# Second pass of a four-layer graph kernel: a fixed order for VectorE and ScalarE over each period of seven products

## The chip, the cores and the metric

The kernel runs on one core of one Trainium2 chip. The metric is the device time of one execution in microseconds (us). Six runs of the kernel before gave 2606.01 to 2609.18, with a median of 2606.47.

## What is computed

The input is `x` (128 x 128 x 256, float32) and one 128 x 128 adjacency matrix. Four layers follow, each of the form `x = x + layer(relu(layernorm(x)))`: a gated graph layer, attention, three graph convolutions, and a layer with two batch norms. The change touches only the second half of the last layer:

```python
agg = jnp.einsum('nm,bmd->bnd', A_hat, features)
x = agg.reshape(-1, d)
h = jax.nn.relu(_batchnorm(x @ W1.T + b1, g1, be1))
out = h @ W2.T + b2
out = _batchnorm(out, g2, be2)
return out.reshape(b, n, -1)
```

Each batch norm needs the mean and variance over all 16384 rows before any row can go on. So the kernel has three stages here: a first pass that ends with `x @ W1.T` of every group, the second pass (normalise, relu, multiply by `W2`, gather statistics) and a final pass (second batch norm, transpose back, add `x`, write out).

## The kernel before

The 128 batches are worked on in 32 groups of four, so that one group is a matrix of 512 rows. After the first pass the pre-activations of 31 groups lie in DRAM as tiles `Z[g]` (128 partitions x 4 chunks x 512 columns), and group 31 is still in SBUF (tiles `zo`). `ORDER` (line 839) is 31, 0, 1, ..., 30. Here n is the place in that order, so n = 0 is group 31 and n = 31 is group 30.

**Loads.** `load_z` (line 843) fetches one group, 1 MB, into one of three buffers `zi` through SyncE's queue. The load for place n+4 is written at the end of place n's turn (line 923) and takes the buffer of place n+1, so it can start only when the last product of place n+1 has read that buffer.

**One group.** `second(g)` (line 859) is a generator, and each `yield` is a step. Four steps apply the first batch norm and the relu in place, one chunk each, on ScalarE (line 868; `relu0` to `relu3`). One step makes sums of quarters of the tile on VectorE (lines 872 to 874). With the quarters a11, a21, a12, a22 these are s1 = a21 + a22, then a21 = a11 - a21, then s2 = s1 - a11, and later, behind product 1, a12 = a12 - s2 (line 884). The matrix product itself is done by a scheme of seven products of half size in place of eight. `seven` (line 412) issues them in the order 0, 1, 4, 5, 2, 6, 3 into three PSUM banks x, y and z:

| step | product into bank | reads | then |
|---|---|---|---|
| 1 | 0 into x | a11 | ScalarE copies x out: `t1` (line 419) |
| 2 | 1 into y | a12 | VectorE a12 = a12 - s2, and the add `o00` = y + t1 (line 894) |
| 3 | 4 into z | s1 | ScalarE copies z out: `t5` (line 419) |
| 4 | 5 onto x | s2 | ScalarE copies x out: `t2` (line 419) |
| 5 | 2 onto z | new a12 | VectorE `o01` = z + t2 |
| 6 | 6 onto x | new a21 | VectorE `o11` = x + t5; half j = 1 is complete: its statistics `S1` (line 897) |
| 7 | 3 onto x | a22 | ScalarE copies the result out: `o10` (line 892); half j = 0 is complete: its statistics `S0` |

Product 5 goes onto bank x and so needs `t1` done; product 2 goes onto z and needs `t5` done; product 6 needs `t2`, and product 3 needs `o11`. A product is four matmul records in the profile (two matmuls of 128 x 256, each in two records), all of line 879.

**Two groups at a time.** The main loop (lines 911 to 925) runs `now`, whose product 0 is already issued, and `then`, the next group. It takes five steps of `now` (products 1, 4, 5, 2, 6) with one preparing step of `then` behind each (four relus, then the sums), then product 0 of `then`, then product 3 of `now`. TensorE's order as written is thus, with a dash for the next group, 1, 4, 5, 2, 6, 0', 3 and again 1', 4', and so on: a period of seven products.

**What sets the order.** The program is written as one stream, and the framework chooses the order of the instructions on each engine when it builds the program: among those whose inputs it takes to be ready, the one that is written first. An engine works through its list in that order, and an instruction that waits holds up all behind it. `tc.keep_in_program_order` puts an instruction behind the one written just before it on the same engine, and adds no wait. In the second pass of the kernel before nothing has it.

**Around it.** `bn_affine` (line 797) turns the statistics into a scale and a shift. For the second batch norm `bn_part` (line 742) aggregates those of the first 31 places into `most2` (line 914, two `BATCH_NORM_AGGREGATE` of line 746), and those of the last place into `last2` (line 936). The final pass (lines 939 to 961) cannot start before both.

Of the kernel before, what the change touches and what calls it, by code (L numbers as in the profile page):

```python
# [9 lines left out]
AF = mybir.ActivationFunctionType  # L10
ALU = mybir.AluOpType
# [11 lines left out]
def kernel(  # L23
# [39 lines left out]
    nc = tc.nc  # L63
    B, N, D = x.shape
    G = 4
    NG = B // G
    T = G * N
    DC = D // P
# [5 lines left out]
    FC = F1 // P  # L74
# [60 lines left out]
    stats2 = const.tile([P, DC, NG, 6], FP, name="stats2")  # L135
# [50 lines left out]
    for v in (b1, g1, be1, b2, g2, be2):  # L186
        k = v.shape[0] // P
# [123 lines left out]
    LAST = NG - 1  # L311
# [100 lines left out]
    def seven(product, put, shape, name, pool=None):  # L412

        def kept(pb, i):
            t = (pool or w).tile(shape, FP, tag="kept", name=f"{name}_t{i}", bufs=6)
            nc.scalar.copy(t, pb)  # L419
            return t  # L420

        px = bank(shape, f"{name}_x")
        product(0, px, True)
        t1 = kept(px, 1)
        yield
        py = bank(shape, f"{name}_y")
        product(1, py, True)
        put((0, 0), py, t1)
        yield
        pz = bank(shape, f"{name}_z")  # L430
        product(4, pz, True)
        t5 = kept(pz, 5)
        yield
        product(5, px, False)
        t2 = kept(px, 2)
        yield
        product(2, pz, False)
        put((0, 1), pz, t2)
        yield
        product(6, px, False)  # L440
        put((1, 1), px, t5)
        yield
        product(3, px, False)
        put((1, 0), px, None)
        yield
# [296 lines left out]
    def bn_part(stats, nch, groups, name):  # L742

        mv = const.tile([P, nch, 2], FP, name=f"mv_{name}")
        for j in range(nch):
            nc.vector.bn_aggr(mv[:, j, :], stats[:, j, groups].rearrange("p g s -> p (g s)"))
        return mv[:, :, 0], mv[:, :, 1]
# [49 lines left out]
    def bn_affine(most, last, nch, gam, bet, name, bias, n):  # L797


        (mean, var), (mean1, var1) = most, last  # L800
        share = n / NG
        d = const.tile([P, nch], FP, name=f"d_{name}")
        nc.vector.tensor_tensor(d, mean1, mean, ALU.subtract)
        nc.vector.scalar_tensor_tensor(mean, d, share, mean, ALU.mult, ALU.add)
        nc.vector.tensor_tensor(mean, mean, bias, ALU.add)
        nc.vector.scalar_tensor_tensor(d, d, share * (1.0 - share), d, ALU.mult, ALU.mult)
        nc.vector.scalar_tensor_tensor(d, var, 1.0 - share, d, ALU.mult, ALU.add)
        nc.vector.scalar_tensor_tensor(var, var1, share, d, ALU.mult, ALU.add)
        sc = const.tile([P, nch], FP, name=f"sc_{name}")
        inv_sqrt(sc, var, BN_EPS)  # L810
        nc.vector.tensor_tensor(sc, sc, gam, ALU.mult)
        sh = const.tile([P, nch], FP, name=f"sh_{name}")
        nc.vector.tensor_tensor(sh, mean, sc, ALU.mult)
        nc.vector.tensor_tensor(sh, bet, sh, ALU.subtract)
        part = const.tile([P, nch], FP, name=f"part_{name}")
        nc.vector.tensor_tensor(part, bias, sc, ALU.mult)
        nc.vector.tensor_tensor(sh, sh, part, ALU.add)
        return sc, sh
# [4 lines left out]
    O = [keep.tile([P, DC, T], FP, name=f"o_{g}") for g in range(NG)]  # L823
# [19 lines left out]
    def load_z(n):  # L843
        z = zin.tile([P, FC, T], FP, tag="zi", name=f"zi_{ORDER[n]}")
        nc.sync.dma_start(z, Z[ORDER[n]])
        ZT[ORDER[n]] = [z[:, :FC // 2, :], z[:, FC // 2 :, :]]

    def load_x3(g, queue=nc.gpsimd):
        k = g % ROOM
        if IN_PASS <= k < IN_Z:  # L850
            if (k - IN_PASS) % 2 == 0:
                pair = zin.tile([P, 2, G, D], FP, tag="zi", name=f"x3i_{g}")
                R[g], R[g + 1] = pair[:, 0], pair[:, 1]
        else:
            pool, tag = (x3p, "x3") if k < OWN else (zp, "z") if k < IN_PASS else (late, "x3l")
            R[g] = pool.tile([P, G, D], FP, tag=tag, name=f"x3i_{g}")
        queue.dma_start(R[g], X3[g].rearrange("(p r) d -> p r d", r=G))

    def second(g):

        zl, zr = ZT[g]
        ex = zw.tile([P, 2, FC // 2, T // 2], FP, tag="zs", name=f"zs_{g}")
        a11, a21, a12, a22 = (z[:, :, i * T // 2 : (i + 1) * T // 2] for z in (zl, zr) for i in range(2))
        s1, s2 = ex[:, 0], ex[:, 1]
        a_r = a11, a12, a12, a22, s1, s2, a21
        for j in range(FC):
            z = ZT[g][j // 2][:, j % 2, :]
            nc.scalar.activation(  # L868
                z, z, AF.Relu, bias=sh1[:, j : j + 1], scale=sc1[:, j : j + 1],
            )  # L870
            yield
        nc.vector.tensor_tensor(s1, a21, a22, ALU.add)
        nc.vector.tensor_tensor(a21, a11, a21, ALU.subtract)
        nc.vector.tensor_tensor(s2, s1, a11, ALU.subtract)
        yield

        def product(r, pb, first):
            for c in range(FC // 2):
                nc.tensor.matmul(  # L879
                    pb, BW2R[r][:, c, :], a_r[r][:, c, :],  # L880
                    start=(first and c == 0), stop=(c == FC // 2 - 1), skip_group_check=True,
                )
            if r == 1:
                nc.vector.tensor_tensor(a12, a12, s2, ALU.subtract)

        done = []

        def put(ij, pb, other):
            i, j = ij
            dst = O[g][:, j, i * T // 2 : (i + 1) * T // 2]  # L890
            if other is None:
                nc.scalar.copy(dst, pb)
            else:
                nc.vector.tensor_tensor(dst, pb, other, ALU.add)
            done.append(j)
            if done.count(j) == 2:
                nc.vector.bn_stats(stats2[:, j, (g + 1) % NG, :], O[g][:, j, :])

        yield from seven(product, put, [P, T // 2], f"po_{g}", zw)

    load_z(1)
# [2 lines left out]
    for n in range(2, 1 + AT_ONCE):  # L904
        load_z(n)
    sc1, sh1 = bn_affine(most1, last1, FC, g1_c, be1_c, "bn1", b1_c, 2)
    PREPARE = FC + 1
    now = second(LAST)
    for _ in range(PREPARE + 1):
        next(now)  # L910
    for n, g in enumerate(ORDER):
        then = second(ORDER[n + 1]) if n + 1 < NG else iter(())
        if n + 1 == NG:
            most2 = bn_part(stats2, DC, slice(LAST), "most2")
        for _ in range(PREPARE):
            next(now)
            next(then, None)
        next(then, None)
        for _ in now:
            pass  # L920
        now = then
        if n + 1 + AT_ONCE < NG:
            load_z(n + 1 + AT_ONCE)
        if n % 4 == 3 and n // 4 < IN_PASS:
            load_x3(n // 4, nc.sync)
# [7 lines left out]

    for g in range(IN_Z, ROOM):
        load_x3(g, nc.sync)
    last2 = bn_part(stats2, DC, slice(LAST, NG), "last2")
    sc2, sh2 = bn_affine(most2, last2, DC, g2_c, be2_c, "bn2", b2_c, 1)
    rows_out = out.rearrange("b (k r) d -> (b k) r d", r=G)
    for g in range(NG):
        x3 = R[g]  # L940
        for i in range(DC):
            nc.scalar.activation(
                O[g][:, i, :], O[g][:, i, :], AF.Identity,
                bias=sh2[:, i : i + 1], scale=sc2[:, i : i + 1],
# [51 lines left out]
```

## Time and profile before

| what | value |
|---|---|
| median of six runs | 2606.47 us |
| the profiled execution's own time | 2606.73 us |
| its span, first to last instruction | 2604.7 us |
| time around the span | 2.0 us |
| TensorE clock granted in the second pass | 1.00 |
| first and last matmul of the second pass (line 879) start | 2330.02 and 2532.57 us |
| records of line 879 | 896 = 32 groups x 7 products x 4 |
| last instruction of VectorE before the final pass ends | 2537.1 us |

The second pass is thus some 203 of the 2605 us. A line of the timeline or of the chain begins with the start and the duration in us. In the timeline follow engine, line of code, operation, what is written and read, the shape and a count, and in brackets the idle time of the engine before it and what ended it. PEld is the loading of weights for a matmul, which may run beside the matmul before it.

### The profile page before, as it was taken

The numbers are of one execution on the slowest core, as the hardware profiler recorded it, in microseconds if no ns is written. First come the engines' busy times: TensorE is split into PE (matmuls) and PEld (weight loads), VectorE is DVE, ScalarE is ACT, GpSimd is POOL, SyncE is SP. The second block draws the span as 40 slices with busy tenths as digits, with TensorE's granted clock in tenths as the row PEclk, the third lists the DMA queues.
The fourth block names the chain that finished last, engine by engine and source line by source line (L and its number), as shares of the span: only waits on it lengthen the run. The fifth ranks groups of instructions, "written<-read, shape, count | busy, mean of one in ns | idle before, by whom it ended". The sixth has DMA issues, their size and how long they took to land.

```text
span 2604.7 us, 40680 instructions
## 1 busy us (share of the span) xinstructions
PE 2539.4 (97%) x15281; PEld 2283.5 (88%) x15281; DVE 1913.8 (73%) x4820; ACT 1283.7 (49%) x2575; POOL 292.1 (11%) x581
## 2 busy tenths in 40 slices
PE   5999999999999999999999999999999999999995
PEld 4899999999999999999999999999999999888875
DVE  6777777777777777777777777777777776567776
ACT  4544454444445544454444444554445444346656
POOL 2110111111110111111111110111011111000001
PEclk8999999999999999999999999999999999999998
DMA  3000000000000000000000000000000000035449
GB/s 133 15 33 33 33 25 25 33 33 34 33 25 25 33 33 33 33 33 17 33 33 33 33 25 25 33 33 33 33 33 25 25 25 25 25 136 181 175 171 394
DMA packets 49560, 143.06 MB, mean 55 GB/s; under 512 B 4162, under 2 KB 23124, under 8 KB 45396
## 3 DMA queue, kind: packets, MB, share of 16 engines
q1 hardware_dynamic: 42164, 116.48, 12.1%
q0 software_dynamic: 6480, 23.60, 2.5%
q8 instruction: 120, 1.97, 0.3%
q14 instruction: 76, 0.62, 0.1%
q10 hardware_dynamic: 720, 0.39, 0.1%
HBM read 73.48 MB, written 66.98 MB: 54 GB/s over the span
## 4 chain that ended last, share of the span: by engine, by line
PE 91%; DMA 3%; DVE 2%; ACT 2%; issue 1%; POOL 1%; ACTq 0%; DVEq 0%; SPq 0%; POOLq 0%
PE p_x L404 17%; PE p_x L387 9%; PE p_z L404 8%; PE pmu L359 4%; PE p_z L387 4%; PE pz_x L404 4%; PE p_y L404 4%; PE pu_x L387 4%; PE po_x L879 3%; PE pg L359 2%; PE ps L577 2%; PE pm L497 2%; PE p_y L387 2%; PE pqv_x L534 2%; PE pr L707 2%; PE py L607 2%
## 5 line engine op out<-in xcount | busy, mean ns | idle before, releaser
L345 ACT ACTIVATE h<-x,sh,rs 128x256 f32<-128x256 f32 x512 | 269.0, 590 | 370.7 <-POOL sh L342 370.7
L404 PE MATMUL p_x<-uT,w 128*128 128x256 f32 x1024 | 242.2, 379 | 0.0
L679 ACT ACTIVATE h2T<-h2T 128x512 f32<-128x512 f32 x192 | 120.6, 628 | 229.0 <-DVE h2T L678 228.5
L404 PEld LDWEIGHTS p_x<-uT,w 128*128 128x128 f32 x1024 | 189.7, 190 | 23.2
L334 DVE BATCH_NORM_STATS2 st<-x 128x6 f32<-128x256 f32 x512 | 191.2, 415 | 3.6 <-DMA x<-in_x_dram 1.5
L338 POOL TENSOR_SCALAR rs<-mv 128x4 f32<-128x4 f32 (+1 forms) x131 | 31.3, 239 | 1394.6 <-ACT h2T L679 1026.7
L456 DVE SCALAR_TENSOR_TENSOR gs<-h,gw 128x256 f32<-128x256 f32 x384 | 161.2, 420 | 33.6 <-ACT h L345 27.6
L419 ACT COPY p_t<-p_x 128x512 f32<-128x512 f32 (+1 forms) x192 | 96.8, 504 | 108.3 <-PE p_x L404 101.5
L339 POOL TENSOR_TENSOR rs<-rs,nhalf 128x4 f32<-128x4 f32 (+1 forms) x131 | 149.7, 1143 | 0.0
L359 PEld LDWEIGHTS pmu<-a2T,u 128*128 128x128 f32 x1024 | 119.4, 192 | 15.3 <-issue 15.1
L387 PEld LDWEIGHTS p_x<-w,h2T 128*128 128x128 f32 x1024 | 124.3, 192 | 3.3
L387 PE MATMUL p_x<-w,h2T 128*128 128x128 f32 x1024 | 124.6, 275 | 0.0
L632 ACT ACTIVATE u<-u 128x512 f32<-128x512 f32 x93 | 58.7, 631 | 133.8 <-DVE u L631 133.8
L868 ACT ACTIVATE zi<-zi,sh_bn,sc_bn 128x512 f32<-128x512 f32 x124 | 97.4, 813 | 49.0 <-DMA zi<-z 39.0
L404 PE MATMUL p_x<-us,w_s 128*128 128x256 f32 x512 | 121.3, 379 | 0.0
L404 PE MATMUL p_z<-us,w 128*128 128x256 f32 x512 | 121.2, 379 | 0.0
L404 PE MATMUL p_x<-uT,w_s 128*128 128x256 f32 x512 | 121.1, 379 | 0.0
L404 PE MATMUL p_y<-uT,w 128*128 128x256 f32 x512 | 121.0, 379 | 0.0
L404 PE MATMUL p_z<-us,w_s 128*128 128x256 f32 x512 | 120.9, 379 | 0.0
L359 PE MATMUL pmu<-a2T,u 128*128 128x128 f32 x1024 | 119.5, 275 | 0.0
L708 DVE TENSOR_TENSOR x<-pr,x 128x512 f32<-128x512 f32 x64 | 43.7, 683 | 90.4 <-PE pr L707 90.4
L404 PEld LDWEIGHTS p_z<-us,w 128*128 128x128 f32 x512 | 97.2, 190 | 13.6 <-ACT p_t L419 0.4
(300 smaller groups left out, 6181.2 us busy)
## 6 DMA issues: line engine op xcount, KB each, us to landing
z<-zo SPq DMA_DIRECT2D x62, 512.0 KB, 2.6
zi<-z SPq DMA_DIRECT2D x31, 1024.0 KB, 4.9
x<-x POOLq DMA_DIRECT2D x32, 512.0 KB, 3.4
x<-in_x_dram SPq DMA_DIRECT2D x31, 512.0 KB, 4.0
out_dram<-x3i SPq DMA_DIRECT2D x30, 512.0 KB, 13.7
x3i<-x SPq DMA_DIRECT2D x19, 512.0 KB, 5.1
x3i<-x POOLq DMA_DIRECT2D x13, 512.0 KB, 11.4
w<-in_L_gnn_W_dram SPq DMA_DIRECT2D x1, 2048.0 KB
```

The lines of the kernel that those rows point to most:

```text
L334: nc.vector.bn_stats(st[:, k, :], xt[:, b, :])
L339: nc.gpsimd.tensor_tensor(rs, rs, nhalf[:, :n], ALU.pow)
L345: nc.scalar.activation(h[:, b, :], xt[:, b, :], AF.Relu, bias=sh[:, k : k + 1], scale=rs[:, k : k + 1])
L359: nc.tensor.matmul(pm[:, k, :], src[:, b, c * P : (c + 1) * P], aT, start=True, stop=True)
L387: nc.tensor.matmul(pb[:, rr, :], a_r[r][:, c, rr * P : (rr + 1) * P], b_r[r][:, c, :wide], start=(first and rr == 0 and c == 0), stop=(c = ...
L404: nc.tensor.matmul(pb[:, jj, :], b_r[r][:, c, at : at + P], a_r[r][:, c, :], start=(first and jj == 0 and c == 0), stop=(c == nk - 1), ski ...
L419: nc.scalar.copy(t, pb)
L456: nc.vector.scalar_tensor_tensor(gs, h[:, b, :], 1.0, gw[:, i, :], ALU.mult, ALU.mult, accum_out=gl[:, k, i : i + 1],)
L632: nc.scalar.activation(dst, dst, AF.Relu)
L679: nc.scalar.activation(dst, dst, AF.Relu)
L868: nc.scalar.activation(z, z, AF.Relu, bias=sh1[:, j : j + 1], scale=sc1[:, j : j + 1],)
L879: nc.tensor.matmul(pb, BW2R[r][:, c, :], a_r[r][:, c, :], start=(first and c == 0), stop=(c == FC // 2 - 1), skip_group_check=True,)
```

## The change

No instruction is added or removed, and first and final pass are untouched. In the second pass:

- The relus, sums, adds, the subtraction behind product 1 and the statistics are kept in program order. The copies `t1`, `t5`, `t2` and `o10` are not marked themselves.
- The order in which they are written is another. Of the next group's preparing steps one relu comes behind product 1, none behind 4, two behind 5, one behind 2, and the sums behind 6 (`AHEAD_AT`).
- The sums are written s1, s2, a21 in place of s1, a21, s2.
- The statistics are put on a list, `TOLD`, and issued by `tell()` behind each step: `S1` directly behind `o11`, and `S0` of the group before behind `o00` of this one. A last `tell()` stands ahead of `last2`.
- `most2` is written behind the first step of the last turn, not ahead of it.

So ScalarE's list over a period reads relu0'', t5', t2', relu1'', relu2'', relu3'', t1'', o10', and VectorE's reads o11, S1, s1', s2', a21', a12', o00', S0, o01' (two dashes: the group after the next).

```diff
+    TOLD = []
+
+    def tell():
+
+        for g, j in TOLD:
+            tc.keep_in_program_order(
+                nc.vector.bn_stats(stats2[:, j, (g + 1) % NG, :], O[g][:, j, :])
+            )
+        TOLD.clear()
+
+    def in_order(*operands):
+        tc.keep_in_program_order(nc.vector.tensor_tensor(*operands))
...
-            nc.scalar.activation(
-                z, z, AF.Relu, bias=sh1[:, j : j + 1], scale=sc1[:, j : j + 1],
+
+            tc.keep_in_program_order(
+                nc.scalar.activation(
+                    z, z, AF.Relu, bias=sh1[:, j : j + 1], scale=sc1[:, j : j + 1],
+                )
             )
             yield
-        nc.vector.tensor_tensor(s1, a21, a22, ALU.add)
-        nc.vector.tensor_tensor(a21, a11, a21, ALU.subtract)
-        nc.vector.tensor_tensor(s2, s1, a11, ALU.subtract)
+        in_order(s1, a21, a22, ALU.add)
+        in_order(s2, s1, a11, ALU.subtract)
+        in_order(a21, a11, a21, ALU.subtract)
...
-                nc.vector.tensor_tensor(a12, a12, s2, ALU.subtract)
+                in_order(a12, a12, s2, ALU.subtract)
...
-                nc.vector.tensor_tensor(dst, pb, other, ALU.add)
+                in_order(dst, pb, other, ALU.add)
             done.append(j)
             if done.count(j) == 2:
-                nc.vector.bn_stats(stats2[:, j, (g + 1) % NG, :], O[g][:, j, :])
+                TOLD.append((g, j))
...
-    PREPARE = FC + 1
+    PREPARE, AHEAD_AT = FC + 1, (1, 0, 2, 1, 1)
...
-        if n + 1 == NG:
-            most2 = bn_part(stats2, DC, slice(LAST), "most2")
-        for _ in range(PREPARE):
+        for k in range(PREPARE):
             next(now)
-            next(then, None)
+            tell()
+            if k == 0 and n + 1 == NG:
+                most2 = bn_part(stats2, DC, slice(LAST), "most2")
+            for _ in range(AHEAD_AT[k]):
+                next(then, None)
         next(then, None)
...
+    tell()
     last2 = bn_part(stats2, DC, slice(LAST, NG), "last2")
```

## The prediction

> **What bounds the kernel now.** I read the page first (one core, clock 1.00 in the second pass), then the matmul start times of line 879, then the waits of 2340 to 2520 us, the timeline of single periods, and the chain.
>
> The busy share says little: TensorE reads as busy all through the pass, because records of 0.38 us overlap. The distance from one record to the next says more. Of 895 distances in the pass, 809 are 0.216 us and the rest longer. The pass takes 895 x 0.2158 = 193.2 us plus 9.4 us of delays. A period of 28 records is 6.04 us without delay, and from the fifth product 4 (2358.08) to the last but one (2520.89) it is on average 162.81 / 26 = 6.26. So TensorE bounds the pass, with 0.22 us per period lost to hand-overs. These are the waits that matter (who waits, for whom, total us, times, longest):
>
> ```profile
> ACT zi L868 <- DMA zi<-z: 39.0, 21, 2.1
> DVE stats L897 <- ACT o L892: 30.7, 27, 1.5
> ...
> PEld po_z L879 <- ACT po_t L419: 7.1, 23, 0.5
> ...
> PEld po_x L879 <- DVE o L894: 5.1, 26, 0.2
> ```
>
> The two large ones lie on engines with time to spare. The two small ones are TensorE's: product 2 (po_z) waits for the copy t5, product 3 (po_x) for the add o11. Here is one such period:
>
> ```profile
> 2502.03 1.03 PE L879 MATMUL po_z<-zs,bw2s_late 128*128 128x256 f32 x4
> 2502.07 1.52 ACT L868 ACTIVATE zi<-zi,sh_bn,sc_bn 128x512 f32<-128x512 f32 x2
> ...
> 2503.49 0.35 ACT L419 COPY po_t<-po_z 128x256 f32<-128x256 f32 x1
> ...
> 2503.90 0.73 PEld L879 LDWEIGHTS po_z<-zi,bw2T 128*128 128x128 f32 x4 [0.39 <-ACT po_t L419]
> 2503.90 1.13 PE L879 MATMUL po_z<-zi,bw2T 128*128 128x256 f32 x4
> ```
>
> Product 4 starts at 2502.03, and two relus sit in front of t5 in ScalarE's list. t5 starts 1.46 us behind product 4, and product 2 comes 1.87 behind it where 8 x 0.216 = 1.73 was possible: 0.14 lost, and 0.10 more inside product 2, whose weights were not loaded ahead. In another period nothing is in front of t5:
>
> ```profile
> 2345.91 1.03 PE L879 MATMUL po_z<-zs,bw2s_late 128*128 128x256 f32 x4
> ...
> 2346.97 0.37 ACT L419 COPY po_t<-po_z 128x256 f32<-128x256 f32 x1 [0.92 <-PE po_z L879]
> ...
> 2347.63 1.03 PE L879 MATMUL po_z<-zi,bw2T 128*128 128x256 f32 x4
> ```
>
> t5 starts at +1.06, and product 2 at +1.72, with no loss. Over all periods in which the order of products held, a t5 up to +1.19 costs nothing, +1.27 costs 0.06, +1.34 costs 0.11, +1.46 costs 0.24. The same holds for o11: at +1.06 behind product 6 (two periods) no loss at product 3, at +1.21 (most periods, behind the sum s2 in VectorE's list) 0.06.
>
> Why the relus stand there, the chain shows:
>
> ```profile
> 2501.39 4.81 DMA zi<-z
> ...
> 2506.29 0.51 ACT zi L868
> 2506.80 0.21 issue
> 2507.01 0.35 ACT po_t L419
> ```
>
> relu0 starts the moment its load lands. The load was issued 1.15 us behind the start of the product 3 that frees its buffer. So there is a loop over two periods: product 3 of n-3, load (5.96 to relu0), four relus with two copies between (3.3), t5 (0.4), product 2 to product 3 of n-1 (2.6). It gives 12.3 / 2 = 6.13, close to the 6.26 seen.
>
> **The change, part by part.** No instruction comes or goes; only places in two lists change. I lay the new lists over a period by rows. Time 0 is the start of product 6; then 0' 0.86, 3 1.73, 1' 2.59, 4' 3.45, 5' 4.32, 2' 5.18, next 6 6.04. A copy or add can start 1.06 after its product starts. Neighbours follow at 0.72 (relu), 0.61 (VectorE, 512 wide), 0.33 (256 wide), 0.72 to 0.79 where one reads the result before it.
>
> *ScalarE*: t1' 1.92, o10 2.79, relu0'' 3.1 to 3.9, t5' 4.51 (nothing ahead since 3.9), t2' 5.38, relu1'' 5.70, relu2'' 6.42, relu3'' to 7.96, t1'' 7.97. So t5 and t2 start at +1.06 in each period. What the order makes late: relu3 ends 0.2 before s1 wants it; relu1 ends (6.52) before product 0'' (6.91). relu0'' now waits for o10, not for the load, which lands at product 3 + 5.9 = 1.6 in this frame, 1.5 ahead of its turn. Queued behind a relu0 that waits would be t5, t2 and all of ScalarE; the cover is those 1.5 us, and a lateness beyond 0.6 more would reach product 2.
>
> *VectorE*: o11 1.06, S1 1.52, s1' 2.13 to 2.82 (product 4' at 3.45), s2' 2.88 to 3.56 (product 5' at 4.32), a21' 3.49, a12' 4.10 to 4.78 (product 2' at 5.18), o00' 4.7, S0 5.03 to 5.72, o01' 6.24 with 0.5 idle before it, o11' 7.10, that is +1.06. S0 no longer waits for o10 (3.15); that wait of 30.7 us cost nothing, as a12 behind it was done 0.3 before product 2. SyncE's queue, the loads and their buffers are as before.
>
> *Sum.* Start: s2 directly behind s1 lets product 5 start at 2333.67, not 2334.18, and product 2 at 2334.82 (a12 done), not 2335.38. The second product 4 comes at 2339.23, not 2339.80: **-0.57**. Then 30 periods at 6.044 are 181.3 us, where the trace has 2527.68 - 2339.80 = 187.9: **-6.57**. The end: the two aggregates of `most2` now stand between S0 and o01 of the last turn.
>
> ```profile
> 2526.56 0.99 DVE L746 BATCH_NORM_AGGREGATE mv_most<-stats 128x2 f32<-128x186 f32 x1
> ...
> 2528.63 0.98 DVE L746 BATCH_NORM_AGGREGATE mv_most<-stats 128x2 f32<-128x186 f32 x1
> ...
> 2531.34 0.42 DVE L894 TENSOR_TENSOR o<-po_x,po_t 128x256 f32<-128x256 f32 x1 [0.37 <-PE po_x L879]
> 2531.82 1.13 PE L879 MATMUL po_x<-zi,bw2s_late 128*128 128x256 f32 x4 [0.52 <-DVE o L894]
> ```
>
> Before, they ended ahead of o00, and o11 started at once (1.06 behind product 6 at 2530.28). Now S0 ends at 5.69, the aggregates at 6.7 and 7.6, o01 starts at 7.54 and o11 at 7.88 in place of 7.10: **+0.79**, as nothing stands between product 6 and product 3 in the last turn. If the builder moves one aggregate forward into idle time, it is nothing. What follows (statistics, `last2`, final pass) keeps its order and starts earlier by as much, its loads too, since they wait for the pass's buffers: one to one.
>
> Sum -6.35, so 2600.4. Pauses that the profile puts down to "issue" (1.57 and 1.42 us on ScalarE, 0.34 on VectorE) now fall into lists with some 0.5 us of room at a time. They cost between nothing, as ScalarE's two did (their periods took 6.13 and 6.18), and 2 us; I take 0.4, near the trace's own case. **-5.9 against the profiled execution's 2606.73: 2600.8**, 5.7 under the median, since that execution lies 0.26 above it.
>
> The Trainium skill ("Runtime: NRT & Kernel Launch", Instruction fetch mechanics) says that instructions are fetched in sequence while earlier ones run, so that the fetch is mostly hidden. If these pauses are fetches, that rule would take nothing for them, and the sum would be 2600.4; the trace's 1.57 us says that not all is hidden.
>
> **Rivals.** 0.2% is 5.2 us, about what a measurement of this kernel can tell from no change.
>
> 1. *One hand-over stays a little late.* t5, t2 and o11 have only 0.13 us between +1.06 and the first loss. If each period keeps one loss of 0.10 (the row of product 2), 30 x 0.10 = 3.0: 2603.8. For it: the thin margin. Against it: t2 started at +1.06 in 27 periods and delayed product 6 in none.
>
> 2. *The gap belongs to the buffers, not to the list.* If a load into a freed buffer stays what ends last, the period stays 6.26: -0.57 + 0.79, 2606.9. For it: relu0 waits for the load in 21 periods. Against it: the loop with one relu ahead of t5 is 5.96 + 0.72 + 0.4 + 2.6 = 9.7 over two periods, less than 12.1. The Trainium skill ("Perfetto Trace Analysis", Optimization Strategy) speaks for this rival: a gap that repeats for a stretch can mean that there is no room for the next tile. The trace agrees that the gap repeats and that the load waits for a buffer; it does not show that the gap needs the buffer.
>
> 3. *Slower: TensorE's own order slips.* The change binds two engines, not TensorE. Where the builder takes product 2's inputs to be late, it puts product 0' of the next group in front, as in the second and fourth periods, where half of 0' came ahead of product 2. If that happens with all of 0' in each period, product 3 follows product 6 directly, as in the last period, and waits 0.68 + 0.10. 30 x 0.78 = 23 on top of 2600.8: 2624. It decides from 0.39 us of loss per period (0.22 as now and 0.17 for 0.2%). Against it: a12 is ready 0.4 before product 2 and t5 earlier than now, and in the steady periods the order held with a later t5.
>
> **How the numbers follow.** Forecast 2600.8, chance 0.70, own range 2599.6 to 2602.2 (aggregate moved forward, no pauses; 1.4 more of pauses); two thirds of it lies under 2601.3, the bound for faster. Rival 1: 0.12. Rival 2: 0.06. Rival 3: 0.08. Anything else: 0.04, half slower. Faster 0.47, same 0.43 (0.23 + 0.12 + 0.06 + 0.02), slower 0.10. The range 2599.4 to 2604.4 holds the forecast and rival 1.
>
> **What would show it.** Right: product 4 to product 4 at 6.04 to 6.06 in nearly all periods; t5, t2 and o11 at +1.06; ScalarE waits for po_x and po_z, no longer for the load; S0 no longer waits for o10; product 6 to product 3 in the last turn 2.3, not 1.54. Wrong: a relu0 that starts as its load lands, a TensorE wait for zs or zi (sums late), or product 0' ahead of 2.

## The result, and the profile after

The kernel after has a median of 2599.70 us (16 runs, 2598.26 to 2601.68), the kernel before on the same chips one of 2606.77 (36 runs). The ratio is 0.9973, interval 0.9966 to 0.9979: 7.1 us less, between 5.5 and 8.9. The profiled execution of after took 2600.27, its span 2598.3.

All of the change is inside the second pass. From its first matmul to the start of its last product 3 the pass took 201.80 us before and takes **195.09** now, 6.71 less. The rest differs too, but by chance: the pass began 1.0 later (2331.02, not 2330.02) and the part behind it was 0.64 shorter. In all fourteen profiled executions of this study the pass began between 2327.8 and 2331.8, with nothing changed ahead of it, and what follows its last product 3 took between 71.6 and 73.0. So below the length of the pass is the measure, and a single whole time carries some 2 us of doubt.

First the waits of after, from 2335 to 2520 us (who waits, for whom, total us, times, longest):

```profile
ACT po_t L419 <- PE po_z L895: 20.2, 31, 1.0
DVE o L870 <- PE po_z L895: 19.2, 30, 0.6
ACT po_t L419 <- PE po_x L895: 15.6, 32, 0.5
ACT o L908 <- PE po_x L895: 14.7, 30, 0.5
DVE o L870 <- PE po_x L895: 11.4, 31, 0.4
DVE o L870 <- ACT zi L883: 1.0, 1, 1.0
PEld po_z L895 <- ACT po_t L419: 0.4, 1, 0.4
```

Of the four lines shown of before, three are gone: no relu waits for a load, no statistic for `o10`, no weight load for `o11`. Of the fourth (7.1 us, 23 times, counted from 2340 us on) one case of 0.4 is left, at 2335.76 in the first group; from 2340 on there is none. In each period ScalarE now waits for TensorE at t5, t2 and `o10`, VectorE at `o01` and `o11`, and TensorE waits for nobody. The matmuls are now line 895, adds and sums 870, statistics 865, relus 883, `o10` 908.

Next the timeline of one period near the end of the pass (start, duration, engine, line, operation, idle time before it):

```profile
2509.40 1.03 PE L895 MATMUL po_z<-zs,bw2s_late 128*128 128x256 f32 x4
...
2510.46 0.37 ACT L419 COPY po_t<-po_z 128x256 f32<-128x256 f32 x1 [0.64 <-PE po_z L895]
...
2511.12 1.03 PE L895 MATMUL po_z<-zi,bw2T 128*128 128x256 f32 x4
...
2511.99 1.89 PE L895 MATMUL po_x<-zi,bw2T 128*128 128x256 f32 x8
...
2513.05 0.42 DVE L870 TENSOR_TENSOR o<-po_x,po_t 128x256 f32<-128x256 f32 x1 [0.37 <-PE po_x L895]
...
2513.71 1.03 PE L895 MATMUL po_x<-zi,bw2s_late 128*128 128x256 f32 x4
...
2515.05 0.81 ACT L883 ACTIVATE zi<-zi,sh_bn,sc_bn 128x512 f32<-128x512 f32 x1
...
2515.44 1.03 PE L895 MATMUL po_z<-zs,bw2s_late 128*128 128x256 f32 x4
...
2516.04 0.68 DVE L870 TENSOR_TENSOR zi<-zi,zs 128x512 f32<-128x512 f32 x1
```

Product 4 follows product 4 at 6.04 (2509.40, 2515.44). The copy t5 starts 1.06 behind product 4 and product 2 comes 1.72 behind it; `o11` starts 1.06 behind product 6 (2511.99), product 3 at +1.72. relu0 follows `o10` and waits for no load. All 30 periods from the second on are 6.04, where before they lay between 6.04 and 6.80.

The shares by engine of the chain that ended last say the same for the whole span; before they were PE 91%, DMA 3%, ACT 2%, issue 1%:

```profile
PE 94%; DVE 2%; DMA 1%; ACT 1%; POOL 0%; issue 0%; ACTq 0%; DVEq 0%; SPq 0%; POOLq 0%
```

### The profile page after: what moved, and what is told of

Same layout as the page of the kernel before. It is cut to its first block, busy times and chain, and to the rows that moved or that the text cites. A ratio compares the mean times of both kernels' runs of the same rounds, so it can differ in the third digit from the quotient of the medians.

```text
span 2598.3 us, 40716 instructions
## 1 busy us (share of the span) xinstructions
PE 2532.9 (97%) x15281; PEld 2287.6 (88%) x15281; DVE 1914.7 (74%) x4820; ACT 1290.9 (50%) x2575; POOL 292.1 (11%) x581
## 4 chain that ended last, share of the span: by engine, by line
PE 94%; DVE 2%; DMA 1%; ACT 1%; POOL 0%; issue 0%; ACTq 0%; DVEq 0%; SPq 0%; POOLq 0%
PE p_x L404 17%; PE p_x L387 9%; PE p_z L404 8%; PE pmu L359 4%; PE p_z L387 4%; PE pz_x L404 4%; PE p_y L404 4%; PE po_x L895 4%; PE pu_x L387 4%; PE pg L359 2%; PE ps L577 2%; PE pm L497 2%; PE p_y L387 2%; PE pqv_x L534 2%; PE pr L707 2%; PE pm L359 2%
## 5 line engine op out<-in xcount | busy, mean ns | idle before, releaser
L404 PEld LDWEIGHTS p_z<-us,w_s 128*128 128x128 f32 x512 | 97.3, 190 | 13.2
```

The costliest lines, as they stand in the source:

```text
L404: nc.tensor.matmul(pb[:, jj, :], b_r[r][:, c, at : at + P], a_r[r][:, c, :], start=(first and jj == 0 and c == 0), stop=(c == nk - 1), ski ...
```

## The experiments

**Theory A** is the prediction's: a period is as long as what stands, on VectorE and on ScalarE, ahead of the copies, adds and sums that TensorE waits for; only an order that is right on both engines reaches 6.04. Its rivals: **B**, the relus on ScalarE are the whole cause; **C**, the statistics that wait on VectorE are; **D**, any fixed order helps, since the builder's choice wavers; **E**, the order in which the program is written does it, without the marks; **F**, every relu ahead of t5 costs time. Rivals 1 to 3 of the prediction have runs as well.

| run | pass us | mean of 30 periods | time (runs) | ratio to before |
|---|---|---|---|---|
| before | 201.80 | 6.263 | 2606.77 (36) | |
| after | 195.09 | 6.043 | 2599.70 (16) | 0.9973 [0.9966, 0.9979] |
| scalar_alone | 207.14 | 6.417 | 2611.82 (10) | 1.0021 [1.0012, 1.0030] |
| vector_alone | 202.25 | 6.261 | 2606.51 (10) | 0.9999 [0.9989, 1.0008] |
| marks_old_places | 207.14 | 6.417 | 2612.27 (10) | 1.0021 [1.0012, 1.0030] |
| new_places_free | 202.18 | 6.276 | 2606.71 (10) | 1.0000 [0.9991, 1.0009] |
| relu_each_step | 195.09 | 6.043 | 2599.16 (1) | |
| two_relus_ahead | 195.09 | 6.043 | 2599.37 (1) | |
| three_relus_ahead | 214.43 | 6.664 | 2620.62 (1) | |
| stats_at_once | 206.88 | 6.417 | 2609.87 (1) | |
| old_sum_order | 197.38 | 6.102 | 2599.61 (1) | |
| four_buffers | 199.61 | 6.190 | 2603.59 (10) | 0.9988 [0.9979, 0.9997] |
| next_product_first | 219.47 | 6.827 | 2622.63 (1) | |
| aggregates_apart | 194.59 | 6.043 | 2597.83 (7) | 0.9970 [0.9959, 0.9981] |

### scalar_alone: only ScalarE's half

The kernel before, with the relus marked and at their new places.

```diff
-            nc.scalar.activation(
+            tc.keep_in_program_order(nc.scalar.activation(
...
-            next(then, None)
+            for _ in range(AHEAD_AT[k]):     # (1, 0, 2, 1, 1)
+                next(then, None)
```

> The kernel before with ScalarE's part alone: relus kept in order and written one, none, two, one (and the sums) behind the steps; VectorE's order is left to the builder, which puts S0 ahead of a12 and s2 behind a21. Theory A (the prediction's: a period is as long as what stands ahead of the copies, adds and sums that TensorE waits for, on both engines): ScalarE's list is that of the changed kernel, so t5 and t2 start at +1.06; but a12 comes at 4.7 to 5.4 behind product 6 (S1, s1, a21, s2, S0 ahead of it) where product 2 wants it at 5.0, so each period loses 0.3 + 0.1: 6.44, and 30 x 0.40 = 12 over the changed kernel, 2612, slower than before. Theory B (ScalarE's relus are the whole cause): 2600 to 2602, period 6.04 to 6.10.

Slower by 5 us, as A said, and B falls: the relus at their new places are not enough. VectorE's list did not stay that of before, though; the builder moved the three sums from ahead of `o11` to behind S1 (what that does, "Why the prediction was right" shows). t5 starts at +1.06 in nearly all periods, as in after, and still the period grew. One turn of the timeline shows for what TensorE waits:

```profile
2439.10 1.89 PE L881 MATMUL po_x<-zi,bw2T 128*128 128x256 f32 x8
...
2443.15 0.69 DVE L899 BATCH_NORM_STATS2 stats<-o 128x6 f32<-128x512 f32 x1
...
2443.75 0.68 DVE L886 TENSOR_TENSOR zi<-zi,zs 128x512 f32<-128x512 f32 x1
...
2444.55 0.73 PEld L881 LDWEIGHTS po_z<-zi,bw2T 128*128 128x128 f32 x4 [0.47 <-issue]
2444.58 1.10 PE L881 MATMUL po_z<-zi,bw2T 128*128 128x256 f32 x4
...
2445.52 1.89 PE L881 MATMUL po_x<-zi,bw2T 128*128 128x256 f32 x8
```

The loop closes on VectorE: product 6 at 2439.10, `a12` at +4.65 with S0 directly ahead of it, product 2 another 0.83 later, the next product 6 another 0.94: 4.65 + 0.83 + 0.94 = 6.42, the measured period. The label "issue" does not name the cause; the times do. In after S0 stands behind `a12` and `o00`, so `a12` starts at +4.05 (2511.99 to 2516.04) and the same loop needs 5.82, less than TensorE's own 6.04.

### vector_alone: only VectorE's half

After, with the relus unmarked.

```diff
-            tc.keep_in_program_order(
-                nc.scalar.activation(
+                nc.scalar.activation(
...
-    PREPARE, AHEAD_AT = FC + 1, (1, 0, 2, 1, 1)
+    PREPARE, AHEAD_AT = FC + 1, (1, 1, 1, 1, 1)
```

> The changed kernel with ScalarE's part undone: relus unmarked and one step of the next group behind each product; VectorE kept in the new order. The builder's list for ScalarE has relu0, t1, relu1, o10, relu2, relu3 ahead of t5 again. Theory A: the loop through the load is back, t5 starts at +1.2 to +1.6 in most periods; only o11 (+1.06) and the start gain: period 6.20, 0.57 + 30 x 0.06 = 2.4 under before, 2604.4. Theory C (VectorE's waits for the statistics were the cause): 2600.

No gain at all, so C falls: the 30 periods take 187.84 us (before 187.88), and the last turn is 0.50 longer, as it is in after. A's size was wrong too, by 2 us: it added up the losses one by one. Two lines of the waits, and one turn of the timeline:

```profile
ACT zi L882 <- DMA zi<-z: 50.0, 25, 2.3
...
PEld po_z L893 <- ACT po_t L419: 9.4, 19, 0.9
```

```profile
2443.91 0.81 ACT L882 ACTIVATE zi<-zi,sh_bn,sc_bn 128x512 f32<-128x512 f32 x1 [2.25 <-DMA zi<-z]
...
2445.41 1.03 PE L893 MATMUL po_z<-zs,bw2s_late 128*128 128x256 f32 x4
...
2447.27 0.36 ACT L419 COPY po_t<-po_z 128x256 f32<-128x256 f32 x1
...
2447.68 0.73 PEld L893 LDWEIGHTS po_z<-zi,bw2T 128*128 128x128 f32 x4 [0.79 <-ACT po_t L419]
```

The load binds. Product 3 at 2437.64 frees the buffer; relu0 of the new group starts at 2443.91 (+6.27); four relus and two copies later comes t5 (+3.36); product 2 (+0.41); product 3 at 2450.38 (+2.70). The sum is 12.74, which is these two periods. This is the prediction's loop, 12.3 there. As long as it ends last, time saved at `o11` only makes t5 later: from the fifth period on it starts up to 1.86 behind product 4, before up to 1.61. So the two losses of before, 0.14 + 0.10 at product 2 and 0.06 at product 3, did not add up: the 0.06 is gone here (the product behind 3 follows at 0.86, not 0.92), and the mean period is as long as it was.

### marks_old_places and new_places_free: the marks and the places apart

The first is the kernel before with every relu, sum, add and statistic marked where it stood. The second is after with all marks taken out.

```diff
 marks_old_places, against before
-            nc.scalar.activation(
+            tc.keep_in_program_order(nc.scalar.activation(
...
-        nc.vector.tensor_tensor(s1, a21, a22, ALU.add)
+        in_order(s1, a21, a22, ALU.add)
...
-                nc.vector.bn_stats(stats2[:, j, (g + 1) % NG, :], O[g][:, j, :])
+                tc.keep_in_program_order(nc.vector.bn_stats(...))
```

```diff
 new_places_free, against after
-            tc.keep_in_program_order(
+            (
                 nc.vector.bn_stats(stats2[:, j, (g + 1) % NG, :], O[g][:, j, :])
...
-        tc.keep_in_program_order(nc.vector.tensor_tensor(*operands))
+        (nc.vector.tensor_tensor(*operands))
...
-            tc.keep_in_program_order(
+            (
                 nc.scalar.activation(
```

> The kernel before with every relu, sum, add and statistic kept in the order in which it was written before: marks without new places. ScalarE's list is relu0, t5, relu1, t2, relu2, relu3, t1, o10; VectorE's is o11, S1, s1, a21, s2, S0, a12, o00, o01. Theory A: a12 as late as with ScalarE's part alone, 6.44 per period, 2612. Theory D (any fixed order frees TensorE, the places matter little): 2600 to 2603.

> The changed kernel with no instruction kept in order: new places without marks. The builder's list for ScalarE is that of the kernel before in the steady periods (relu0, t1, relu1, o10, relu2, relu3, t5, t2). Theory A: period 6.2 to 6.27 as before, t5 late, 2605 to 2607. Theory E (the order in which it is written is enough): 2600.

Both as A said. Marks at the old places give the same 207.14 as scalar_alone, for the same reason (the sums behind S1 and S0 ahead of `a12`), so D falls. New places without marks give before's time, since the builder goes back to nearly before's order: E falls. The gain needs the right places, held.

### relu_each_step, two_relus_ahead, three_relus_ahead: how much may stand ahead of a copy

After, with other places for the relus.

```diff
-    PREPARE, AHEAD_AT = FC + 1, (1, 0, 2, 1, 1)
+    PREPARE, AHEAD_AT = FC + 1, (1, 1, 1, 1, 1)   # relu_each_step
+    PREPARE, AHEAD_AT = FC + 1, (2, 0, 1, 1, 1)   # two_relus_ahead
+    PREPARE, AHEAD_AT = FC + 1, (3, 0, 0, 1, 1)   # three_relus_ahead
```

> The changed kernel with one relu behind each of products 1, 4, 5 and 2 (1, 1, 1, 1, 1): ScalarE's list is relu0, t5, relu1, t2, relu2, relu3, t1, o10, with VectorE as changed. Theory A: relu1 runs from 4.84 to 5.66 behind product 6, so t2, ready at 5.38, starts at +1.22 to +1.28 behind product 5; by the rows of t5 that costs 0.02 to 0.07 per period at product 6: period 6.06 to 6.11, 1 to 2 us over the changed kernel. Theory F (only the number of relus ahead of t5 counts): 6.04, no difference.

> The changed kernel with two relus ahead of t5 (2, 0, 1, 1, 1). Theory A: relu0 starts at 3.1 (behind o10), relu1 ends at 4.7, t5 starts at 4.55 to 4.6, that is +1.10, under the +1.19 that costs nothing: period 6.04, no difference to the changed kernel. Theory F (each relu ahead of t5 costs its 0.72): period 6.04 + 0.6, 18 us more.

> The changed kernel with three relus ahead of t5 (3, 0, 0, 1, 1). The builder answers with another order on TensorE: 4, 5, all of 0', half of 1', 2, 6, the other half of 1', 3. Theory A: t5 starts 0.77 late, which the products put in front of 2 hide; but only half a product stands between 6 and 3, so 3 waits 0.3 for o11 and 0.06 to 0.10 more inside: period 6.35 to 6.45, 9 to 12 us over the changed kernel. If the load or the relus bind instead, the waits of line 883 name it.

With two relus ahead of t5 the period stays 6.04, so F falls. With one relu between t5 and t2 the copy t2 starts at +1.19 in 31 of 32 turns, and product 6 is not late: A had feared 1 to 2 us, and the run confirms instead that +1.19 is free, as the trace of before had it for t5.

With three ahead, t5 starts at +2.24 to +2.32 and the pass is 19.3 us longer than after's, not 9 to 12. A had the wait for `o11` (the second line); it left out the one for s1 (the first):

```profile
PEld po_z L895 <- DVE zs L870: 14.3, 26, 0.6
...
PEld po_x L895 <- DVE o L870: 6.3, 13, 0.5
```

The builder is free on TensorE and puts product 0' ahead of product 2 in nearly every period, and half of 1' in every second one, while t5 is late. That hides t5, but product 4 then comes sooner behind product 3 and waits for s1, and where half of 1' went ahead, product 3 comes sooner behind product 6 and waits for `o11`. The periods take 6.48 and 6.85 by turns. A late copy moved the loss to two other hand-overs.

### stats_at_once and old_sum_order: parts of VectorE's half undone

After, with S0 issued as soon as it is written, ahead of `a12`; and after with the sums as before.

```diff
 stats_at_once
                 TOLD.append((g, j))
+                if j == 0:
+                    tell()
 old_sum_order
         in_order(s1, a21, a22, ALU.add)
-        in_order(s2, s1, a11, ALU.subtract)
         in_order(a21, a11, a21, ALU.subtract)
+        in_order(s2, s1, a11, ALU.subtract)
```

> The changed kernel with S0 issued behind its own product 3, not behind o00 of the next group: on VectorE it stands ahead of a12, its input o10 long ready. Nothing else differs. Theory A: a12 moves from 4.10-4.78 to 4.71-5.39 behind product 6, product 2 wants it at 5.0: 0.3 + 0.1 per period, 6.44, 12 us over the changed kernel. Theory B (statistics are off the path, ScalarE's order is the whole cause): 6.04, no difference.

> The changed kernel with the sums written s1, a21, s2 as before. Theory A: product 5 of the first group starts 0.5 later (the start's gain is gone); in the steady periods s2 ends at 4.15 behind product 6 (product 5 wants it at 4.17) and a12 at 4.9 (product 2 wants it at 5.0): between no loss and 0.06 per period, so 0.5 to 2.5 us over the changed kernel, in the pass.

One early S0 takes away the whole gain and more: 6.417, the same loop as in scalar_alone to the last digit. One turn shows it:

```profile
2441.69 0.69 DVE L865 BATCH_NORM_STATS2 stats<-o 128x6 f32<-128x512 f32 x1
...
2442.15 0.37 ACT L419 COPY po_t<-po_z 128x256 f32<-128x256 f32 x1 [0.64 <-PE po_z L895]
2442.29 0.67 DVE L870 TENSOR_TENSOR zi<-zi,zs 128x512 f32<-128x512 f32 x1
...
2443.08 0.73 PEld L895 LDWEIGHTS po_z<-zi,bw2T 128*128 128x128 f32 x4 [0.51 <-ACT po_t L419]
2443.11 1.10 PE L895 MATMUL po_z<-zi,bw2T 128*128 128x256 f32 x4
```

The bracket blames t5, which ended at 2442.52, more than 0.5 us before. What ends last is `a12`, at 2442.96; product 2 follows its start by 0.82, as in scalar_alone by 0.83.

The order of the sums is worth 2.29 us of the pass: 0.26 in the start, 1.77 in the periods (28 of 6.08 or 6.09, two of 6.37), 0.26 in the last turn. In the two long periods `a12` starts 0.35 later than in the others (4.59 behind product 6, not 4.24), which the profile puts down to TensorE; why is open. The whole time, 2599.61, hides this loss, because this execution's pass began 3.2 us earlier than after's.

### four_buffers: rival 2

The kernel before, with a fourth buffer for the loads (and, to make room, two tiles fewer for the final pass).

```diff
-    OWN, IN_PASS, IN_Z, ROOM = 6, 8, 14, 19
+    OWN, IN_PASS, IN_Z, ROOM = 4, 6, 14, 19
...
-        tc.tile_pool(name="zin", bufs=3, side="right", reuse_waits="tile")
+        tc.tile_pool(name="zin", bufs=4, side="right", reuse_waits="tile")
...
-    AT_ONCE = 3
+    AT_ONCE = 4
```

> The kernel before with four buffers for the loads of the second pass in place of three (and two tiles fewer for the final pass, to make room). Rival 2 of the prediction (the gap belongs to the buffers): relu0 no longer starts as its load lands, the period falls to 6.04 to 6.1, and the pass is 4 to 6 us shorter with the lists left to the builder. The other reading (the gap belongs to the lists): the relus run earlier, but still stand ahead of t5, and s2 ahead of o11: period 6.15 to 6.27. The final pass may move by itself; the verdict is on the pass.

A third of the gain: 2.2 of 6.7 us of the pass.

```profile
ACT zi L868 <- DMA zi<-z: 14.6, 8, 2.1
...
PEld po_z L879 <- ACT po_t L419: 4.9, 12, 0.6
```

The waits for the load went from 39.0 us to 14.6, TensorE's wait for t5 only from 7.1 to 4.9. The builder's lists changed with the buffers: two relus stand directly ahead of t5 in 14 turns and one in 14 others, where before it was two in 28. So the buffers are a part of the loop, but the gap goes without a fourth one.

### next_product_first: rival 3, enforced by marks

After, with the matmuls marked too and product 0' ahead of product 6, the sums behind S1.

```diff
-                nc.tensor.matmul(
+                tc.keep_in_program_order(nc.tensor.matmul(
...
-    PREPARE, AHEAD_AT = FC + 1, (1, 0, 2, 1, 1)
+    PREPARE, AHEAD_AT = FC + 1, (2, 0, 1, 3, 0)
```

> The changed kernel with TensorE's order kept by marks too, and with product 0 of the next group ahead of product 6 (1, 4, 5, 2, 0', 6, 3): rival 3 of the prediction, enforced. Two relus stand ahead of t5 so that product 0' has its input. Theory A: product 3 waits for o11 directly behind product 6, 0.68 and 0.10 per period as in the last turn: period 6.82, 23 us over the changed kernel, 2623. If the order of TensorE did not matter: no difference.

The price of rival 3 was right: 6.827 per period, 0.78 more than after, and 2622.6 in all. The wait is the one it named, `o11` between products 6 and 3:

```profile
PEld po_x L904 <- DVE o L870: 24.8, 27, 0.9
```

### aggregates_apart: the end of the pass

After has one loss left, in the last turn (next section). Here each of the last two turns has one aggregate, kept in order behind S0. `most2` then covers 30 places and `last2` two.

```diff
-            if k == 0 and n + 1 == NG:
-                most2 = bn_part(stats2, DC, slice(LAST), "most2")
+            if k == 0 and n + 2 >= NG:
+                j = NG - 1 - n
+                tc.keep_in_program_order(
+                    nc.vector.bn_aggr(
+                        mv2[:, j, :], stats2[:, j, : LAST - 1].rearrange("p g s -> p (g s)")
+                    )
+                )
...
-    last2 = bn_part(stats2, DC, slice(LAST, NG), "last2")
+    last2 = bn_part(stats2, DC, slice(LAST - 1, NG), "last2")
```

> The changed kernel with the two aggregates of most2 apart: one in the last turn but one, one in the last, each kept behind S0 and ahead of o01, where VectorE's list has 0.5 idle; most2 covers 30 places and last2 two. Theory A: o01 starts 0.4 late, which no one waits for, and the last turn loses nothing: product 4 of the last place to its product 3 takes 4.14, not 4.63: 0.5 us less than the changed kernel, which is within what a measurement of the whole kernel can tell.

The last turn is back at 4.13, and the pass 0.50 shorter than after's. Its median of 2597.83 is the lowest of all and 1.9 under after's, but only the 0.50 is shown to be its own: of the 3.0 between the two profiled executions, 2.2 are an earlier start of the pass, and the intervals of the two ratios overlap.

## Why the prediction was right

| term | predicted | measured in after |
|---|---|---|
| start, to the second product 4 | -0.57 | -0.62 (6.99 to 6.37) |
| 30 periods | -6.57 | -6.58 (187.88 to 181.30) |
| end, last product 4 to product 3 | +0.79 | +0.50 (4.13 to 4.63) |
| pauses | +0.4 | 0 |
| sum | -5.9 | -6.71 |

The forecast of 2600.8 lies 0.5 above the profiled execution (2600.27) and 1.1 above the median. The terms were off by a little more: the pass gained 0.8 more than forecast, as the end and the pauses had been put too dear. That the whole time came closer is luck, since the pass happened to begin 1.0 later and the rest to be 0.64 shorter.

**The periods.** Every place in the two lists that was laid out by rows is where it was put: t5, t2 and `o11` at +1.06, relu0 behind `o10`. The load landed at 2489.41 and its relu0 started at 2490.87, 1.46 ahead of need, where 1.5 was forecast. That VectorE *and* ScalarE had to be laid out was the point: ScalarE's half alone gives +5.34 us in the pass, VectorE's +0.45, both together -6.71.

**What the prediction had not seen.** It took t5 and `o11` for the two losses, and S0's wait for free. For the lists of before that was right: S0 stood directly ahead of `a12` in 31 of 32 groups, and `a12` was still done 0.4 before product 2 in most of them. But it was free only because the three sums (lines 872 to 874) ran ahead of `o11`. One turn of before:

```profile
2434.60 0.68 DVE L872 TENSOR_TENSOR zs<-zi 128x512 f32<-128x512 f32 x1
2435.31 0.69 DVE L873 TENSOR_TENSOR zi<-zi 128x512 f32<-128x512 f32 x1
...
2436.36 0.68 DVE L874 TENSOR_TENSOR zs<-zs,zi 128x512 f32<-128x512 f32 x1
2436.96 0.42 DVE L894 TENSOR_TENSOR o<-po_x,po_t 128x256 f32<-128x256 f32 x1
2437.41 0.69 DVE L897 BATCH_NORM_STATS2 stats<-o 128x6 f32<-128x512 f32 x1
2439.58 0.69 DVE L897 BATCH_NORM_STATS2 stats<-o 128x6 f32<-128x512 f32 x1 [1.48 <-ACT o L892]
2440.19 0.68 DVE L884 TENSOR_TENSOR zi<-zi,zs 128x512 f32<-128x512 f32 x1
```

Product 6 starts at 2435.74 here, and `a12` at +4.45; in no period of before does it start later. With the relus at their new places the sums can't run there: s1 needs relu3, which ends behind the start of `o11` (2513.81 against 2513.05 in after). All three sums come behind S1, and with S0 still ahead of `a12` this makes +4.65 and a period of 6.42 (scalar_alone; in marks_old_places and stats_at_once marks put the sums and S0 there). So ScalarE's new places need S0's new place: of VectorE's new order it is the part on which the most hangs (11.8 us of the pass against after), then the order of the sums (2.3).

**The end** was mis-sized, and its mechanism was another. The prediction had both aggregates between S0 and `o01`, so that `o11` and product 3 would be late (2.3 from product 6). The builder, to which the aggregates are free, moved one of them forward between s1 and s2. The timeline of the last turn of after:

```profile
2520.17 0.67 DVE L870 TENSOR_TENSOR zs<-zi 128x512 f32<-128x512 f32 x1
...
2520.76 0.98 DVE L746 BATCH_NORM_AGGREGATE mv_most<-stats 128x2 f32<-128x186 f32 x1
...
2521.48 1.03 PE L895 MATMUL po_z<-zs,bw2s_late 128*128 128x256 f32 x4
...
2521.66 0.63 DVE L870 TENSOR_TENSOR zs<-zs,zi 128x512 f32<-128x512 f32 x1
...
2522.40 0.73 PEld L895 LDWEIGHTS po_x<-zs,bw2s_late 128*128 128x128 f32 x4 [0.30 <-issue]
2522.43 1.10 PE L895 MATMUL po_x<-zs,bw2s_late 128*128 128x256 f32 x4
...
2522.80 0.68 DVE L870 TENSOR_TENSOR zi<-zi,zs 128x512 f32<-128x512 f32 x1
...
2523.60 0.73 PEld L895 LDWEIGHTS po_z<-zi,bw2T 128*128 128x128 f32 x4 [0.47 <-issue]
2523.63 1.10 PE L895 MATMUL po_z<-zi,bw2T 128*128 128x256 f32 x4
...
2524.57 1.03 PE L895 MATMUL po_x<-zi,bw2T 128*128 128x256 f32 x4
...
2526.11 1.13 PE L895 MATMUL po_x<-zi,bw2s_late 128*128 128x256 f32 x4 [0.52 <-DVE o L870]
```

s2 starts 1.49 behind s1, not 0.71, so product 5 comes 0.95 behind product 4 (0.86 without delay), product 2 comes 1.20 behind product 5, 0.83 behind `a12`, and product 6 another 0.94: 0.09 + 0.34 + 0.08 = 0.51 late. Product 6 to product 3 is 1.54, as before, so the predicted sign of 2.3 was wrong. The prediction allowed for a builder that moves an aggregate forward, but took that for free.

**Pauses.** Nothing in the periods of after is longer than 6.05, so no pause cost anything. The Trainium skill ("Runtime: NRT & Kernel Launch", Instruction fetch mechanics) says that sequential fetch is mostly hidden; by that rule the sum was 2600.4. The trace of after, without an "issue" pause between 2335 and 2520 us, does not speak against it; whether the pauses of before were fetches no run here shows.

**The rivals.** 1: no hand-over stays late; +1.06 to +1.19 is free (relu_each_step). 2: the gap of 0.22 per period went with three buffers, by order alone. The Trainium skill ("Perfetto Trace Analysis", Optimization Strategy) says that a gap that repeats can mean a lack of room for the next tile; here a fourth buffer took 0.07 of the 0.22 (6.263 to 6.190), the order with three buffers all of it. 3: the builder kept product 6 ahead of 0' in all periods; enforced in next_product_first, the slip costs what was said (0.78 per period).

## What to carry to other kernels

Where TensorE is the bound and two other engines hand it tiles, close each loop on paper by start times, one per engine and one per buffer; the longest sets the period, and losses inside the same loop do not add up. A fixed order is only as good as its worst place: held in the wrong places it cost 5 us, held in the right ones it gained 7, and without the marks the right places did nothing. When one hand-over gets better, ask what stays free to move, here the aggregates and TensorE's own list.

## What had not been expected of the hardware

- A copy that can start at 1.06 behind its product may start a little later at no cost: t2 started at +1.19 in 31 of 32 turns of relu_each_step, and the product that reuses its bank still followed at +1.73.
- Where a weight load came late, the loss had two parts: the wait, and the distance from that product to the next, which was 0.94 (scalar_alone) or 0.97 (most periods of before) in place of 0.86.
- On VectorE a 512-wide operation follows its neighbour at 0.60 to 0.61, one that reads its neighbour's result at 0.71 (s1 2514.12, s2 2514.83, a21 2515.44 in after) or 0.78 (s2 to `a12` in old_sum_order).
- The bracket on a late weight load can name an engine long done, or "issue", where the real releaser was `a12` on VectorE (scalar_alone, stats_at_once); only the constant 0.82 to 0.83 from `a12`'s start to product 2 gave it away.
